# Self-attention's queries and keys as seven half products per two pairs of heads and two batches, with slots in twos

## The chip, the cores and the metric

The kernel runs on one core of one Trainium2 chip. The metric is the device time of one execution in microseconds. The core has five instruction streams: TensorE (PE; its weight loads are listed apart as PEld), VectorE (DVE), ScalarE (ACT), GpSimd (POOL) and SyncE (SP), which issues the DMAs. Each stream runs its instructions in order; an instruction that depends on another engine waits for a semaphore.

## The reference

One decoder block on x of 8 batches, 224 rows, 512 columns, in float32:

1. self-attention: x is RMS-normalised, multiplied by Wq and Wkv (512 to 1024 each for queries, keys and values), split into 16 heads of 64. Queries and keys are divided by their norm over the head's 64 columns and scaled by a gamma. Scores go through tanh(s/50)*50/8 and a softmax over 224 keys, then the weighted values through Wo; x plus the result is layer-normalised.
2. cross-attention to a context of 750 rows, and a layernorm.
3. a gated feed-forward with rounded activations and three-valued weights, and a layernorm.

Only self-attention's queries and keys change here:

```
q = x @ Wq;  k = x @ Wk            # x: normalised, 512 columns; Wq, Wk: 512 x 1024
q = q / max(norm(q), 1e-12) * (gamma_q + 1) * 8   # per head of 64, the same for k
```

## The kernel before, in words

x lives in SBUF as 14 tiles of 128 rows. Self-attention works on groups g of two batches (448 columns of the transposed x, `xnT`; four groups) and on pairs of heads hp (128 columns of Wq or Wk; eight pairs), so on 32 slots m = 8g + hp. All engines but SyncE run in an order that is written out by hand (`manual_schedule`); SyncE's DMAs are placed by the framework where their buffers come free.

One slot m of the loop records, in this order: the weighted values of the slot before (`self_values(m - 1)`: 16 instructions on TensorE, then one multiply on VectorE, L426, into oT); the scores (`self_scores(m)`: 16 on TensorE, then tanh and exp on ScalarE into the two tiles `prs`); `scale_qk(m + 1)` on VectorE (two transposes L313, two multiplies L315); `project_qk(m + 2)` (L263: 32 TensorE instructions of 448 columns, since each float32 matmul stands as two instructions in the trace; ScalarE copies the result and squares it, L287 and L288); `inverse_sums(m)` on VectorE, in two parts (L373 to L404: the softmax's sums and their reciprocals); between its parts `head_norms(m + 2)` (L290: a reduce of the squares L295, four copies L302, two small operations L305 and L306 on VectorE into the tile `nm_q`, then a reciprocal root on GpSimd, L129, into `nm_i`); a value projection (`project_v`, L320) where one is due; a transposition of the normalised x and its copy into xnT (L254, L258) for the next group; an output product through Wo of the group before (`self_output`, L446, and its addition L455 on VectorE); layernorms of what became complete; and the squares, mean squares and scaling of x for the next group.

Buffers that matter: `nm_q` and `nm_o` have one buffer each; `nm_i`, `sq_qk` and other tiles without a number have two; `qk` three. PSUM has three banks under the tag "mm", shared by the projections, the transposed x and the outputs, two double banks for the scores and one bank for the weighted values (`ov_a`). The weights pool has four slots: Wq, Wk, Wv and Wo; at m = 29 the cross-attention's weights are loaded into slots that have come free.

A slot's names in the prediction: Q is `scale_qk`, H is `head_norms`, I is `inverse_sums`, M is the multiply L426. Two slots 2p and 2p + 1 are pair p.

Of the kernel before, what the change touches and what calls it, by code (L numbers as in the profile page):

```python
# [20 lines left out]
F32 = mybir.dt.float32  # L21
BF16 = mybir.dt.bfloat16
AF = mybir.ActivationFunctionType
# [39 lines left out]
def decoder_block(ctx: ExitStack, tc: tile.TileContext, a: dict, out: bass.AP):  # L63
# [47 lines left out]
    wq, wk, wv = ws  # L111
    for i in range(NX // 2, NX):
        load_x(i)
    wo = load_w("attn_Wo", INNER // P, DIM)

    ident = const.tile([P, P], F32, name="ident")
    make_identity(nc, ident)
# [9 lines left out]
    def rsqrt(y, v):  # L127

        nc.gpsimd.tensor_tensor(  # L129
            y, v, mhalf.to_broadcast([P, v.shape[-1]]), ALU.pow  # L130
        )
# [85 lines left out]
    with tc.tile_pool(name="a_sb", bufs=2) as sb, tc.tile_pool(  # L217
# [8 lines left out]
        trs, mms = {}, {}  # L226
# [29 lines left out]
        def copy_xn(i):  # L256
# [3 lines left out]
                ALU.mult,  # L260
            )

        def project_qk(m):  # L263

            for w in range(2):
                block_qk(m, w, (0, G))

        def block_qk(m, w, cols):

            g, hp = divmod(m, NPAIR)  # L270
            c0, c1 = cols
            if (w, c0) == (0, 0):
                qk[m] = sb.tile([P, 2, G], F32, name="qk", bufs=3)
                sq_qk[m] = sb.tile([P, 2, G], F32, name="sq_qk")
            if c0 == 0:
                mms[w] = ps_mm.tile([P, G], F32, tag="mm", name="mm_qk")
            mm = mms[w]
            for k in range(KD):
                nc.tensor.matmul(  # L279
                    mm[:, c0:c1],  # L280
                    lhsT=(wq, wk)[w][:, k, hp * P : (hp + 1) * P],
                    rhs=xnT[:, k, g % 2 * G + c0 : g % 2 * G + c1],
                    start=(k == 0),
                    stop=(k == KD - 1),
                )
            if c1 == G:
                nc.scalar.copy(qk[m][:, w], mm)  # L287
                nc.scalar.activation(sq_qk[m][:, w], qk[m][:, w], AF.Square)  # L288

        def head_norms(m):  # L290

            quarter = sb.tile([P, 4 * NB], F32, name="nm_q", bufs=1)
            nc.vector.tensor_reduce(  # L295
                quarter, sq_qk[m].rearrange("p w (b c) -> p (w b) c", c=Q32), AX.X, ALU.add,
                apply_transpose=True,
            )
# [7 lines left out]
            nc.vector.tensor_scalar(quarter, quarter, 1e-24, None, ALU.max)  # L306
            inv[m] = sb.tile([P, 2, 2 * NB, 1], F32, name="nm_i")
            rsqrt(inv[m].rearrange("p w b o -> p (w b o)"), quarter)

        def scale_qk(m):  # L310
            rb, r = sq_qk.pop(m), inv.pop(m)
            for w in range(2):
                nc.vector.transpose(rb[:, w], r[:, w].to_broadcast([P, 2 * NB, Q32]))  # L313
            for w in range(2):
                nc.vector.scalar_tensor_tensor(  # L315
                    qk[m][:, w], qk[m][:, w], gscale[:, w, m % NPAIR, :], rb[:, w],
                    ALU.mult, ALU.mult,
                )

# [16 lines left out]

        def self_scores(m):

            qT, kT = qk[m][:, 0], qk[m][:, 1]
            scs = []  # L340
            for u in range(2):
                sc = ps_sc.tile([P, 2, 512], F32, name="sc_a")
                sc = sc[:, :, 0 : NT * S].rearrange("p j (t q) -> p j t q", t=NT)
                scs.append(sc)
                for kt, (k0, n) in enumerate(KEYS):
                    for j in range(2):
                        h0, c = j * DH, u * S
                        nc.tensor.matmul(  # L348
                            sc[:n, j, kt, :],
                            lhsT=kT[h0 : h0 + DH, c + k0 : c + k0 + n],  # L350
                            rhs=qT[h0 : h0 + DH, c : c + S],
                            start=True,
                            stop=True,
                        )
# [12 lines left out]

        def inverse_sums(m):


            quarter = sb.tile([P, 2, 2, NB, NT, P // Q32], F32, name="sm_q", bufs=1)
            for u in range(2):
                nc.vector.tensor_reduce(  # L373
                    quarter[:, u, :, :, :, 0].rearrange("p j b t -> p j t b"),
                    prs[u].rearrange("p j t (b c) -> p j t b c", c=Q32),
                    AX.X, ALU.add, apply_transpose=True,
                )


            flat = quarter.rearrange("p u j b t g -> p (u j b t) g")  # L380
            for g in range(1, P // Q32):
                nc.vector.tensor_copy(
                    flat[:Q32, :, g], flat[g * Q32 : (g + 1) * Q32, :, 0]
                )
            yield
            tot = sb.tile([Q32, 2, 2, NB], F32, name="sm_t", bufs=1)
            nc.vector.tensor_reduce(
                tot.rearrange("p u j b -> p (u j b)"),
                quarter[:Q32].rearrange("p u j b t g -> p (u j b) (t g)"), AX.X, ALU.add,
            )  # L390
            isum = sb.tile([P, 2, 2 * NB, 1], F32, name="sm_i", bufs=1)
            for j in range(2):
                nc.vector.reciprocal(
                    isum[:Q32, j, :, 0].rearrange("p (u b) -> p u b", u=2), tot[:, :, j]
                )
            for g in range(1, P // Q32):
                nc.vector.tensor_copy(
                    isum[g * Q32 : (g + 1) * Q32, g // 2, :, 0],
                    isum[:Q32, g // 2, :, 0],
                )  # L400
            rcs[m] = sb.tile([P, 2, S], F32, name="rc_a", bufs=1)
            for j in range(2):
                half = slice(j * DH, (j + 1) * DH)
                nc.vector.transpose(  # L404
                    rcs[m][half].rearrange("p u q -> p (u q)"),
                    isum[half, j].to_broadcast([DH, 2 * NB, Q32]),
                )
            yield

        def self_values(m):  # L410
            g, hp = divmod(m, NPAIR)
# [72 lines left out]
        project_v(0, 0)  # L484
        project_v(1, 0)
        project_qk(1)
        scale_qk(0)
        head_norms(1)
        for i in opened[0][2:]:
            project_v(i, 0)  # L490

        out_at = [(), (0, 2, 4), (0, 2, 4, 6), (4, 5, 6)]
        for m in range(NS):
            g, hp = divmod(m, NPAIR)
            if m > 0:
                self_values(m - 1)
            self_scores(m)
            for i in due:
                scales.append(layernorm([i]))
            due.clear()  # L500
            if m + 1 < NS:
                scale_qk(m + 1)
            if m + 2 < NS:
                project_qk(m + 2)
            sums = inverse_sums(m)
            next(sums)
            if m + 2 < NS:
                head_norms(m + 2)

            c = 1 - hp // 4  # L510
            tiles = opened[g + hp // 4] if g + hp // 4 < NG else ()
            if hp % 4 < len(tiles):
                project_v(tiles[hp % 4], c)
            for _ in sums:
                pass
            for f in scales:
                f()
            scales.clear()
            ahead = opened[g + 1] if g + 1 < NG else ()
# [10 lines left out]
            if 1 <= hp < 1 + len(ahead):  # L530
                scale_x(ahead[hp - 1])
# [22 lines left out]
    dram = ctx.enter_context(tc.tile_pool(name="dram", bufs=1, space=bass.MemoryType.DRAM))  # L554
# [658 lines left out]
```

## Time and profile before

| | before |
|---|---|
| median of 3 runs | 1692.4 us (1692.2 to 1693.05) |
| profiled execution, its own time | 1693.18 us |
| its span, first to last instruction | 1691.4 us |
| granted TensorE clock | 0.999 |
| scores of slot 0 / of slot 31 start | 39.05 / 486.10 us |
| scores to scores, m = 4 to 5, 5 to 6 | 13.47, 13.03 us |
| busy from 38.5 to 143 us: PE, DVE, ACT, POOL | 104.5, 80.1, 65.0, 37.7 of 104.5 us |

A line of the order of time reads: start in us, length, engine, line, operation, output <- input with their shapes, count; in brackets the idle time of the engine just before, and what ended it. Matmuls overlap, so the length of one is not its spacing; the spacing is read from the starts of successive blocks.

### The profile page before, as it was taken

What the parts mean: (1) busy time and instruction counts of PE and PEld (TensorE: products, weight loads), DVE (VectorE), ACT (ScalarE), POOL (GpSimd) and SP (SyncE); (2) the same over time, 40 slices, a digit from 0 to 9 for tenths busy, and PEclk for the clock granted to TensorE, in tenths of its full rate; (3) what the DMA queues carried; (4) which work ended last, traced back from release to release, by engine and by line L of the source; (5) the groups of instructions that cost most, each with busy time, mean ns of one, the idle gap of its engine ahead of it and who ended that gap; (6) DMA issues with size and microseconds to landing.
All of it is one profiled execution on the core that took longest, in us unless ns stands there. A gap on an engine that the chain in (4) does not pass through costs nothing.

```text
span 1691.4 us, 23310 instructions
## 1 busy us (share of the span) xinstructions
PE 1674.4 (99%) x8602; PEld 1076.8 (64%) x8602; DVE 1247.2 (74%) x2776; ACT 879.1 (52%) x1492; POOL 628.9 (37%) x507
## 2 busy tenths in 40 slices
PE   8999999999999999999999999999999999999998
PEld 4555554555546777776776776776776776774443
DVE  3777776767865776776886886897875776886877
ACT  4655544545523664654664664563453544445663
POOL 3333332333411443443443443443443443443244
PEclk9999999999999999999999999999999999999999
DMA  8000000000133222211221121110000000031333
GB/s 286 1 1 1 1 1 1 1 1 1 38 115 109 76 99 75 75 35 38 69 72 38 54 87 38 36 43 7 1 29 3 4 28 1 1 150 30 71 83 105
DMA packets 61956, 80.47 MB, mean 48 GB/s; under 512 B 36753, under 2 KB 38801, under 8 KB 59409
## 3 DMA queue, kind: packets, MB, share of 16 engines
q1 hardware_dynamic: 61840, 78.97, 14.5%
q8 instruction: 68, 1.11, 0.3%
q14 instruction: 48, 0.39, 0.1%
HBM read 60.34 MB, written 9.96 MB: 42 GB/s over the span
## 4 chain that ended last, share of the span: by engine, by line
PE 97%; DVE 1%; DMA 1%; issue 0%; SPq 0%; POOL 0%; POOLq 0%; DVEq 0%
PE mm_k L748 15%; PE mm_v L736 15%; PE mm_qk L279 12%; PE sc_c L785 9%; PE ov_c L879 9%; PE mm_o L446 6%; PE mm_q L761 6%; PE mm_co L194 6%; PE mm_v L325 6%; PE mm_f L1014 5%; PE sc_a L348 3%; PE ov_a L418 3%; PE dn L1102 2%; DMA cT<-ctxT 1%; PE tr_x L254 0%; PE tr_x L719 0%
## 5 line engine op out<-in xcount | busy, mean ns | idle before, releaser
L869 POOL TENSOR_TENSOR csh<-cpT 125x672 f32<-125x672 f32 x128 | 207.4, 1621 | 577.8 <-DVE cpT L859 552.0
L867 ACT ACTIVATE cpT<-cpT 125x1344 f32<-125x1344 f32 x128 | 169.6, 1325 | 228.9 <-DVE cpT L859 220.1
L748 PE MATMUL mm_k<-cT,xattn_Wk 128*128 128x375 f32 x768 | 258.5, 485 | 1.2 <-DMA cT<-ctxT 1.1
L736 PE MATMUL mm_v<-xattn_Wv,cT 128*125 128x256 f32 x1152 | 259.1, 379 | 0.0
L129 POOL TENSOR_TENSOR nm_i<-nm_q,mhalf 128x28 f32<-128x28 f32 x32 | 153.2, 4786 | 271.1 <-DVE nm_q L306 262.5
L736 PEld LDWEIGHTS mm_v<-xattn_Wv,cT 128*125 128x125 f32 x1152 | 216.3, 188 | 28.9
L793 ACT COPY cpT<-sc_c 125x448 f32<-125x448 f32 x384 | 173.7, 561 | 104.2 <-PE sc_c L785 104.1
L748 PEld LDWEIGHTS mm_k<-cT,xattn_Wk 128*128 128x128 f32 x768 | 140.0, 189 | 101.0 <-issue 12.2
L859 DVE TENSOR_TENSOR cpT<-cpT,mx_b 125x1344 f32<-125x1344 f32 x128 | 193.2, 1550 | 2.2
L795 DVE TENSOR_TENSOR cm<-sc_c,cpT 125x448 f32<-125x448 f32 x128 | 73.9, 619 | 146.5 <-ACT cpT L793 146.5
L785 PE MATMUL sc_c<-cqT,ckT 64*125 64x224 f32 x1536 | 163.1, 358 | 0.0
L879 PE MATMUL ov_c<-cpT,cv 125*64 125x224 f32 x1536 | 159.4, 357 | 0.0
L785 PEld LDWEIGHTS sc_c<-cqT,ckT 64*125 64x125 f32 x1536 | 140.3, 184 | 24.7 <-ACT ckT L755 15.0
L879 PEld LDWEIGHTS ov_c<-cpT,cv 125*64 125x64 f32 x1536 | 104.6, 137 | 47.3 <-issue 18.2
L755 ACT COPY ckT<-mm_k 128x375 f32<-128x375 f32 x128 | 59.2, 462 | 126.1 <-PE mm_k L748 126.1
L358 ACT ACTIVATE pr<-sc_a 128x448 f32<-128x448 f32 (+1 forms) x128 | 61.8, 536 | 91.2 <-PE sc_a L348 91.1
L279 PE MATMUL mm_qk<-xnT,wq 128*128 128x448 f32 (+2 forms) x280 | 107.0, 527 | 1.5 <-DVE xnT L258 1.4
L761 PE MATMUL mm_q<-xT,xattn_Wq 128*128 128x224 f32 x512 | 107.1, 352 | 0.0
L761 PEld LDWEIGHTS mm_q<-xT,xattn_Wq 128*128 128x128 f32 x512 | 96.7, 189 | 16.3
L279 PE MATMUL mm_qk<-xnT,wk 128*128 128x448 f32 x256 | 101.5, 539 | 0.0
L325 PE MATMUL mm_v<-wv,xnT 128*128 128x512 f32 x224 | 100.4, 592 | 0.0
L1014 PE MATMUL mm_f<-ternary,xqT 128*128 128x512 bf16 x448 | 98.7, 379 | 0.9 <-DVE x L906 0.9
(131 smaller groups left out, 2530.2 us busy)
## 6 DMA issues: line engine op xcount, KB each, us to landing
cT<-ctxT SPq DMA_DIRECT2D x8, 1125.0 KB, 5.3
w_stage<-w_gateT SPq DMA_DIRECT2D x8, 1024.0 KB, 4.9
w_stage<-w_upT SPq DMA_DIRECT2D x8, 1024.0 KB, 5.1
w_stage<-w_downT SPq DMA_DIRECT2D x8, 1024.0 KB, 5.2
tern<-w_t SPq DMA_DIRECT2D x24, 256.0 KB, 2.0
ternary<-tern SPq DMA_DIRECT2D x3, 2048.0 KB, 12.4
x<-x SPq DMA_DIRECT2D x14, 256.0 KB, 7.4
out<-x SPq DMA_DIRECT2D x14, 256.0 KB, 2.3
```

What stands on the lines that cost most here:

```text
L279: nc.tensor.matmul(mm[:, c0:c1], lhsT=(wq, wk)[w][:, k, hp * P : (hp + 1) * P], rhs=xnT[:, k, g % 2 * G + c0 : g % 2 * G + c1], start=(k = ...
L325: nc.tensor.matmul(mm, lhsT=xnT[:, k, at : at + P], rhs=wv[:, k, c * 512 : (c + 1) * 512], start=(k == 0), stop=(k == KD - 1),)
L736: nc.tensor.matmul(mm[:, i, :], lhsT=cT[:, k, c * CT : (c + 1) * CT], rhs=xwv[:, k, g * VN : (g + 1) * VN], start=(k == 0), stop=(k == KC ...
L748: nc.tensor.matmul(mm, lhsT=xwk[:, k, hp * P : (hp + 1) * P], rhs=cT[:, k, c * HALF : (c + 1) * HALF], start=(k == 0), stop=(k == KC - 1),)
L761: nc.tensor.matmul(mm, lhsT=xwq[:, k, hp * P : (hp + 1) * P], rhs=xT[:, k, :], start=(k == 0), stop=(k == KD - 1),)
L785: nc.tensor.matmul(sc[j][:, i, :], lhsT=kT[h0 : h0 + DH, ct * CT : (ct + 1) * CT], rhs=qT[h0 : h0 + DH, :], start=True, stop=True,)
L793: nc.scalar.copy(pT[:, j, 2 * c2 : 2 * c2 + 2, :], sc[j])
L859: nc.vector.tensor_tensor(pT[:, j], pT[:, j], nm[:CT, j] .rearrange("p (o q) -> p o q", o=1) .to_broadcast([CT, NCT, S]), ALU.add,)
L867: nc.scalar.activation(pT[:, j], pT[:, j], AF.Exp)
L869: nc.gpsimd.tensor_tensor(half, pT[:, j, 0:3], pT[:, j, 3:6], ALU.add)
L879: nc.tensor.matmul(ov[h0 : h0 + DH, :], lhsT=v[:, ct, hq * DH : (hq + 1) * DH], rhs=pT[:, j, ct, :], start=(ct == 0), stop=(ct == NCT - 1),)
L1014: nc.tensor.matmul(mm, lhsT=xqTs[i][:, k, :], rhs=w[:, k, cols], start=(k == 0), stop=(k == KD - 1),)
```

## The change

The products of two pairs of heads (2 x 128 columns of Wq and of Wk) with the two batches of a group are computed as a block product: the contraction of 512 is halved (2 x 256), the weights are halved by the pair of heads, the input by the batch. A 2 x 2 block product by Winograd's form needs seven block products in place of eight, with four sums of weight blocks and four sums of input blocks, and additions of the products. Some of the additions are made in PSUM (a bank `mx` that goes on accumulating after it has been copied out), three on VectorE (`add`, from a second bank `mz`). For each pair j of pairs of heads and group:

- `project_pair(j)` replaces `project_qk(2j)` and `project_qk(2j + 1)`, in five pieces, which the loop puts between the other work of an even slot. The first pair of group 0 is still made as before.
- qk and sq_qk are laid out by batch, then query or key; qk has four buffers.
- `sum_input(g)` makes the four input sums (for group 0 on VectorE, for the others on GpSimd), `sum_weights(jj)` the four weight sums of Wq and of Wk (one set on VectorE, three on GpSimd), and writes them to DRAM.
- In groups 1 to 3 the blocks of a pair are loaded by `load_pair(j)` into one tile, with the sums from DRAM: six DMAs of 128 KB and two of 512 KB each time. Wo is loaded in slot 4 in place of the start.
- Slots go in twos: `scale_qk` runs twice in an even slot, `head_norms` twice in an odd slot, and `inverse_sums` is no longer in parts. In group 1 and 2 the outputs move by a slot, and so do the transpositions.

```diff
-    wo = load_w("attn_Wo", INNER // P, DIM)
+    dram = ctx.enter_context(tc.tile_pool(name="dram", bufs=1, space=bass.MemoryType.DRAM))
...
+        work = wpool.tile([P, 2, 2, 4, KD // 2, P], F32, tag="w", name="w_sums")
+        sums_w = dram.tile([P, NPAIR // 2, 2, 4, KD // 2, P], F32, name="w_sums_all")
+        sums_x = sb.tile([P, 4, KD // 2, S], F32, name="x_sums", bufs=1)
...
+        def sum_weights(jj, eng):
+            for w in range(2):
...
+                eng.tensor_tensor(s1, a21, a22, ALU.add)
+                eng.tensor_tensor(s2, s1, a11, ALU.subtract)
+                eng.tensor_tensor(s3, a11, a21, ALU.subtract)
+                eng.tensor_tensor(s4, a12, s2, ALU.subtract)
+            nc.sync.dma_start(out=sums_w[:, jj], in_=work[:, jj % 2])
...
+        def sum_input(g, eng):
+            b11, b12, b21, b22 = input_blocks(g)
+            t1, t2, t3, t4 = (sums_x[:, i] for i in range(4))
+            eng.tensor_tensor(t1, b12, b11, ALU.subtract)
+            eng.tensor_tensor(t2, b22, t1, ALU.subtract)
+            eng.tensor_tensor(t3, b22, b12, ALU.subtract)
+            eng.tensor_tensor(t4, b21, t2, ALU.subtract)
...
+        def project_pair(j):
+            m = 2 * j
+            open_qk(m)
+            open_qk(m + 1)
+            w = blocks(j)
...
+            yield
+            mx = ps_mm.tile([P, 2, S], F32, tag="mm", name="mm_x")
+            mz = ps_mm.tile([P, 2, S], F32, tag="mm", name="mm_z")
+            def product(mm, first, left, right):
+                for i in range(2):
+                    for k in range(KD // 2):
+                        nc.tensor.matmul(
+                            mm[:, i],
+                            lhsT=w[i][left][:, k],
+                            rhs=right[:, k],
+                            start=first and (i, k) == (0, 0),
+                            stop=(k == KD // 2 - 1),
+                            skip_group_check=True,
+                        )
+            def square_qk(n, u):
+                nc.scalar.activation(sq_qk[n][:, u], qk[n][:, u], AF.Square)
+            def add(n, u):
+                y = qk[n][:, u]
+                nc.vector.tensor_tensor(y, mz, y, ALU.add)
+            product(mx, True, 0, b11)
+            nc.scalar.copy(qk[m][:, 0], mx)
+            product(mz, True, 1, b21)
+            add(m, 0)
+            yield
+            product(mx, False, 4, t2)
+            nc.scalar.copy(qk[m][:, 1], mx)
+            square_qk(m, 0)
+            product(mz, True, 3, t1)
+            product(mx, False, 5, t3)
+            nc.scalar.copy(qk[m + 1][:, 1], mx)
+            yield
+            add(m + 1, 1)
+            yield
+            product(mx, False, 2, t4)
+            nc.scalar.copy(qk[m + 1][:, 0], mx)
+            square_qk(m + 1, 1)
+            square_qk(m + 1, 0)
+            product(mz, False, 6, b22)
+            add(m, 1)
+            square_qk(m, 1)
+            yield
...
         project_qk(1)
+        sum_input(0, nc.vector)
         scale_qk(0)
+        sum_weights(1, nc.vector)
         head_norms(1)
...
-        out_at = [(), (0, 2, 4), (0, 2, 4, 6), (4, 5, 6)]
+        out_at = [(), (1, 3, 5), (1, 3, 5, 6), (4, 5, 6)]
         for m in range(NS):
             g, hp = divmod(m, NPAIR)
+            even = m % 2 == 0
+            pair = project_pair(m // 2 + 1) if even and m + 2 < NS else None
+            step = (lambda: next(pair)) if pair else (lambda: None)
+            step()
+            step()
+            if even and m > 0:
+                scale_qk(m)
             if m > 0:
                 self_values(m - 1)
+            step()
             self_scores(m)
             for i in due:
                 scales.append(layernorm([i]))
             due.clear()
-            if m + 1 < NS:
+            if even:
                 scale_qk(m + 1)
-            if m + 2 < NS:
-                project_qk(m + 2)
-            sums = inverse_sums(m)
-            next(sums)
-            if m + 2 < NS:
+            elif m + 1 < NS:
+                head_norms(m + 1)
                 head_norms(m + 2)
+            step()
+            step()
+            inverse_sums(m)
...
-            for _ in sums:
-                pass
...
-            if 2 <= hp < 2 + len(ahead):
-                transpose_xn(ahead[hp - 2])
-                copy_xn(ahead[hp - 2])
+            if 1 <= hp < 1 + len(ahead):
+                transpose_xn(ahead[hp - 1])
+                copy_xn(ahead[hp - 1])
...
+            if g == 0 and hp in (0, 2, 4):
+                sum_weights((2, 3, 0)[hp // 2], nc.gpsimd)
+            if ahead and hp == 4:
+                sum_input(g + 1, nc.gpsimd)
+            if m >= 4 and even and m + 4 < NS:
+                load_pair(m // 2 + 2)
+            if m == 4:
+                wo = load_w("attn_Wo", INNER // P, DIM)
```

More of the change, by code (lines that the diff above doesn't have):

```diff
@@ L225, in decoder_block @@
         rms_rs = stat.tile([P, NX], F32, name="rms_rs", bufs=1)
-        trs, mms = {}, {}
+        work = wpool.tile([P, 2, 2, 4, KD // 2, P], F32, tag="w", name="w_sums")
+        sums_w = dram.tile([P, NPAIR // 2, 2, 4, KD // 2, P], F32, name="w_sums_all")
+        sums_x = sb.tile([P, 4, KD // 2, S], F32, name="x_sums", bufs=1)
+        trs, mms, loaded = {}, {}, {}
         xn, qk, sq_qk, inv, v, oT, rcs = {}, {}, {}, {}, {}, {}, {}
@@ L261, in copy_xn, with open_qk @@
             )
+        def open_qk(m):
+            qk[m] = sb.tile([P, 2, 2, S], F32, name="qk", bufs=4)
+            sq_qk[m] = sb.tile([P, 2, 2, S], F32, name="sq_qk")
         def project_qk(m):
@@ L268, in block_qk @@
         def block_qk(m, w, cols):
-            g, hp = divmod(m, NPAIR)
             c0, c1 = cols
             if (w, c0) == (0, 0):
-                qk[m] = sb.tile([P, 2, G], F32, name="qk", bufs=3)
-                sq_qk[m] = sb.tile([P, 2, G], F32, name="sq_qk")
+                open_qk(m)
             if c0 == 0:
@@ L280, in block_qk @@
                     mm[:, c0:c1],
-                    lhsT=(wq, wk)[w][:, k, hp * P : (hp + 1) * P],
-                    rhs=xnT[:, k, g % 2 * G + c0 : g % 2 * G + c1],
+                    lhsT=(wq, wk)[w][:, k, m * P : (m + 1) * P],
+                    rhs=xnT[:, k, c0:c1],
                     start=(k == 0),
@@ L286, in block_qk, with blocks @@
             if c1 == G:
-                nc.scalar.copy(qk[m][:, w], mm)
-                nc.scalar.activation(sq_qk[m][:, w], qk[m][:, w], AF.Square)
+                y = qk[m][:, :, w, :]
+                nc.scalar.copy(y, mm.rearrange("p (u q) -> p u q", u=2))
+                nc.scalar.activation(sq_qk[m][:, :, w, :], y, AF.Square)
+        def blocks(j):
+            g, jj = divmod(j, NPAIR // 2)
+            if g:
+                w7 = loaded.pop(j)
+                return [[w7[:, w, i] for i in range(7)] for w in range(2)]
+            return [
+                [
+                    (wq, wk)[w][:, 2 * kh : 2 * kh + 2, (2 * jj + i) * P : (2 * jj + i + 1) * P]
+                    for i, kh in ((0, 0), (0, 1), (1, 1))
+                ]
+                + [work[:, jj % 2, w, i] for i in range(4)]
+                for w in range(2)
+            ]
@@ new lines, in sum_weights @@
+        def sum_weights(jj, eng):
+            for w in range(2):
+                a11, a12, a21, a22 = (
+                    (wq, wk)[w][:, 2 * kh : 2 * kh + 2, (2 * jj + i) * P : (2 * jj + i + 1) * P]
+                    for i in range(2)
+                    for kh in range(2)
+                )
+                s1, s2, s3, s4 = (work[:, jj % 2, w, i] for i in range(4))
+                eng.tensor_tensor(s1, a21, a22, ALU.add)
[3 more added lines that the diff above has]
+            nc.sync.dma_start(out=sums_w[:, jj], in_=work[:, jj % 2])
@@ new lines, in load_pair @@
+        def load_pair(j):
+            jj = j % (NPAIR // 2)
+            if not loaded.get("tile"):
+                loaded["tile"] = [wpool.tile([P, 2, 7, KD // 2, P], F32, tag="w", name="w_pair")]
+            w7 = loaded[j] = loaded["tile"][0]
+            for w, (name, at) in enumerate((("attn_Wq", 0), ("attn_Wkv", 0))):
+                src = a[name].rearrange("(k p) n -> p k n", p=P)
+                for n, (i, kh) in enumerate(((0, 0), (0, 1), (1, 1))):
+                    c = at + (2 * jj + i) * P
+                    nc.sync.dma_start(
+                        out=w7[:, w, n], in_=src[:, 2 * kh : 2 * kh + 2, c : c + P]
+                    )
+                nc.sync.dma_start(out=w7[:, w, 3:], in_=sums_w[:, jj, w])
@@ new lines, in input_blocks @@
+        def input_blocks(g):
+            c = g % 2 * G
+            return [
+                xnT[:, 2 * kh : 2 * kh + 2, c + u * S : c + (u + 1) * S]
+                for kh in range(2)
+                for u in range(2)
+            ]
+        def sum_input(g, eng):
[5 more added lines that the diff above has]
+            eng.tensor_tensor(t4, b21, t2, ALU.subtract)
@@ new lines, in project_pair @@
+        def project_pair(j):
+            m = 2 * j
+            open_qk(m)
+            open_qk(m + 1)
+            w = blocks(j)
+            b11, _, b21, b22 = input_blocks(j // (NPAIR // 2))
+            t1, t2, t3, t4 = (sums_x[:, i] for i in range(4))
+            yield
[11 more added lines that the diff above has]
+                            skip_group_check=True,
+                        )
+            def square_qk(n, u):
[25 more added lines that the diff above has]
+            yield
@@ L295, in head_norms @@
             nc.vector.tensor_reduce(
-                quarter, sq_qk[m].rearrange("p w (b c) -> p (w b) c", c=Q32), AX.X, ALU.add,
-                apply_transpose=True,
+                quarter, sq_qk[m].rearrange("p u w (b c) -> p (u w b) c", c=Q32), AX.X,
+                ALU.add, apply_transpose=True,
             )
@@ L307, in head_norms @@
             inv[m] = sb.tile([P, 2, 2 * NB, 1], F32, name="nm_i")
-            rsqrt(inv[m].rearrange("p w b o -> p (w b o)"), quarter)
+            rsqrt(inv[m].rearrange("p u b o -> p (u b o)"), quarter)
         def scale_qk(m):
             rb, r = sq_qk.pop(m), inv.pop(m)
-            for w in range(2):
-                nc.vector.transpose(rb[:, w], r[:, w].to_broadcast([P, 2 * NB, Q32]))
+            for u in range(2):
+                nc.vector.transpose(
+                    rb[:, u].rearrange("p w q -> p (w q)"),
+                    r[:, u].to_broadcast([P, 2 * NB, Q32]),
+                )
             for w in range(2):
                 nc.vector.scalar_tensor_tensor(
-                    qk[m][:, w], qk[m][:, w], gscale[:, w, m % NPAIR, :], rb[:, w],
+                    qk[m][:, :, w], qk[m][:, :, w], gscale[:, w, m % NPAIR, :], rb[:, :, w],
                     ALU.mult, ALU.mult,
@@ L337, in self_scores @@
         def self_scores(m):
-            qT, kT = qk[m][:, 0], qk[m][:, 1]
             scs = []
@@ L346, in self_scores @@
                     for j in range(2):
-                        h0, c = j * DH, u * S
+                        head = qk[m][j * DH : (j + 1) * DH, u]
                         nc.tensor.matmul(
                             sc[:n, j, kt, :],
-                            lhsT=kT[h0 : h0 + DH, c + k0 : c + k0 + n],
-                            rhs=qT[h0 : h0 + DH, c : c + S],
+                            lhsT=head[:, 1, k0 : k0 + n],
+                            rhs=head[:, 0, :],
                             start=True,
@@ L384, in inverse_sums @@
                 )
-            yield
             tot = sb.tile([Q32, 2, 2, NB], F32, name="sm_t", bufs=1)
@@ L407, in inverse_sums @@
                 )
-            yield
         def self_values(m):
@@ L529, in decoder_block @@
                     rms_norms(ahead[0], ahead[-1] + 1)
-            if 1 <= hp < 1 + len(ahead):
-                scale_x(ahead[hp - 1])
+            if hp < len(ahead):
+                scale_x(ahead[hp])
+            if g == 0 and hp in (0, 2, 4):
[6 more added lines that the diff above has]
+                wo = load_w("attn_Wo", INNER // P, DIM)
             if m == NS - 3:
@@ L553, in decoder_block @@
     parts = const.tile([P, 3, NCHUNK], F32, name="w_parts")
-    dram = ctx.enter_context(tc.tile_pool(name="dram", bufs=1, space=bass.MemoryType.DRAM))
     ternary = [dram.tile([P, NCHUNK, CHUNK], BF16, name=f"tern{i}") for i in range(3)]
```

## The prediction

> **What bounds the kernel now.** I read the busy shares first, then the chain of work that ended last, then TensorE's list of waits up to 530 us, and last the order of time of VectorE and GpSimd in two ordinary slots of self-attention. The page's first part and its chain:
>
> ```profile
> PE 1674.4 (99%) x8602; PEld 1076.8 (64%) x8602; DVE 1247.2 (74%) x2776; ACT 879.1 (52%) x1492; POOL 628.9 (37%) x507
> ...
> PE 97%; DVE 1%; DMA 1%; issue 0%; SPq 0%; POOL 0%; POOLq 0%; DVEq 0%
> ```
>
> TensorE is the end's owner nearly everywhere. Its waits list names 8.5 us over all of self-attention, 7.7 of them before 9 us, so a slot costs what its matmuls cost. VectorE is second, and its stretch of one slot (m=5, start, length, engine, line) shows how little room it has:
>
> ```profile
> 106.74 0.61 DVE L426 TENSOR_TENSOR oT<-ov_a,rc_a 128x448 f32<-128x448 f32 x1
> 108.51 1.17 DVE L313 STREAM_TRANSPOSE sq_qk<-nm_i 128x448 f32<-128x448 f32 x2 [1.16 <-POOL nm_i L129]
> 109.60 1.24 DVE L315 SCALAR_TENSOR_TENSOR qk<-qk,gscale,sq_qk 128x448 f32<-128x448 f32 x2
> 110.76 2.10 DVE L373 TRANSPOSE_TENSOR_REDUCE sm_q<-pr 128x28 f32<-128x896 f32 x2
> 112.89 0.65 DVE L382 COPY sm_q<-sm_q 32x56 f32<-32x56 f32 x3
> 114.70 1.11 DVE L295 TRANSPOSE_TENSOR_REDUCE nm_q<-sq_qk 128x28 f32<-128x896 f32 x1 [1.16 <-ACT sq_qk L288]
> ...
> 116.83 0.18 DVE L306 TENSOR_SCALAR nm_q<-nm_q 128x28 f32<-128x28 f32 x1
> 116.92 0.37 DVE L387 TENSOR_REDUCE sm_t<-sm_q 32x28 f32<-32x224 f32 x1
> ...
> 118.25 1.31 DVE L404 STREAM_TRANSPOSE rc_a<-sm_i 64x448 f32<-64x448 f32 x2
> 119.67 0.62 DVE L426 TENSOR_TENSOR oT<-ov_a,rc_a 128x448 f32<-128x448 f32 x1
> ```
>
> From start to start I take VectorE's pieces: Q (scale_qk) 110.76−108.51 = 2.25; H (head_norms) 116.92−114.70 = 2.2; I (inverse_sums) 2.13+0.66+2.7 = 5.5; M (the multiply of oT) 0.6. That is 10.6 of a 13.0 us slot, and 10.6 of 9.6 us in a slot without project_v, where it falls behind a little and catches up later. GpSimd's order of time gives the length of one reciprocal root (L129) and what follows it:
>
> ```profile
> 117.15 4.78 POOL L129 TENSOR_TENSOR nm_i<-nm_q,mhalf 128x28 f32<-128x28 f32 x1 [8.49 <-DVE nm_q L306]
> 121.89 0.24 POOL L431 COPY oT_tail<-oT 128x64 f32<-128x64 f32 x1
> ```
>
> It starts 0.14 us after H's last instruction ends (117.01), lasts 4.78, and Q starts 0.04 later (121.97): 5.0 us from the end of H to anyone who waits for the root.
>
> [...] Here a 224-column matmul (L761) lasts 352 ns but takes 5.7% of the chain for 512, 188 ns each, the length of its weight load (189); a 448-column one is spaced 375. So halving the columns halves the time, with nothing to spare. [...] L869 (672 elements, 1621 ns) and L870 (224, 667) give 1.14 us for 448 and 0.75 for 256.
>
> **The change, part by part.** *Products.* Two slots' queries and keys were 2 x 32 instructions of 448 columns, 6.12 us a slot (107.21 to 113.33). Now 7 products of 8 instructions of 224 columns: 56 x 188 = 10.53 us. Saved 12.24−10.53 = 1.71 a pair of slots, 25.6 over the 15 pairs changed (pair 0 stays). This alone would give 1667.
>
> *Additions on VectorE.* Three of 128x448 with a PSUM operand, as L426, 0.62 each: 1.9 us a pair. ScalarE keeps four copies and four squares a pair.
>
> *Input and weight sums.* At the start on VectorE, 4 x 0.62 and 8 x about 0.42 (L896, 224 elements, 0.39): they fit into VectorE's 4.9 us of waiting for the root before 27.8 us and 3.3 before 33.5. Uncovered they'd cost 6. On GpSimd three times 8 x 0.75 = 6 us and three times 4 x 1.14 = 4.6; its queue holds H's root behind them. At m=0, 2, 4 and 20 they are done before H ends; at m=12 they wait for the last copy of x and push the root out by 1.8.
>
> *Transfers.* Eight a pair, 1.8 MB; as cT (1125 KB, 5.3 us) some 10 us for the lot. The last two start when the seventh product ends and are wanted about 25 us later. SP's queue holds only the next loads and Wo and xattn_Wk behind them. Nothing, or up to 10 us a pair if late.
>
> *The order.* This decides. In an odd slot head_norms now runs twice in a row. Its tile nm_q has one buffer, and GpSimd's root reads it. So the second H's reduce waits until the first root is done; the built program carries this wait (VectorE's L428 on GpSimd's L129). VectorE stands for 5.0 us, with I(odd), and all after it, behind. Before, Q, I's first half and a whole slot lay between. And TensorE's third product overwrites mm_z, which the first addition A1 must have read: A1 stands behind I(odd).
>
> That closes a ring. From A1's end: 0.1, two products 3.0, scores 1.7, two products 3.0, 0.05 (the last addition needs the seventh product): 7.85. Then on VectorE: addition 0.6, I 5.5, M 0.6, H 2.2, wait 5.0, H 2.2, I 5.5, A1 0.6. Sum 30.05 us a pair. TensorE's own sum with project_v in both slots is 10.53 + scores and values 6.76 + 2 x 3.53 = 24.35, so the ring leads unless an output (6.87) is in the pair.
>
> Added to the ring where they occur: copy of x from the transposition (L258) 0.69, layernorm's scale 0.55, the output's addition 0.69. At m=0, 8, 16 VectorE's mean-square line waits for ScalarE's squares of x, done at 11.4, 12.8 and 11.4 us from the scores' start against 10.9: 0.6, 2.1, 0.6. In slots 9, 11, 17, 19 a transposition and an output follow each other, and with three PSUM buffers the second product gets the one that the transposed x held, so it waits for that copy, which stands after I(odd): then 7.7 us of TensorE (two products' remains, values, three products) come behind it. The layernorm statistics hide in the 2 us before the last addition. In pair 22/23 the output stands in the even slot, and M comes only after it, at 17 us instead of 11; in 28/29 at 13.4.
>
> Scores to scores, pair by pair: 31.4, 31.5, 30.1, 30.1; 37.1, 36.0, 33.7, 30.6; 35.5, 36.0, 31.5, 37.6; 30.1, 30.1, 33.5; the last slot 10.25. Sum 505. The first scores start at 46.6 instead of 39.05 (five products of the first pair now go ahead of them). So the last scores start at 551.6; before at 486.1. What follows is unchanged. +65.5 on the profiled execution (1693.2, span 1691.4): 1758.7; on the median 1692.4: 1757.9. The TensorE gain is inside it: it is swallowed.
>
> **Rivals.** (2) The ring holds but its extras lie in other waits: each pair costs the greater of 30.1 and TensorE's sum (31.8, 31.8, 31.8, 32.2, 31.3 where outputs are). Sum 470, last scores at 517, 1723. For it: I placed each wait by hand. Against: each stands in the in-order queue. (3) VectorE gets slower beside a busier GpSimd, or the weights of a pair come late: some 2 us a pair more, 1775 to 1800. L404 takes 1.31 us both beside a root of GpSimd (118.25) and without one (at 494 us), which speaks against the first. (4) The second H doesn't wait for GpSimd: ring 25.1, and the same list sums to 440.6, last scores at 487.2: 1693.5, no change. (5) The other side: TensorE keeps the lead, 1667. Its one mechanism: the second norm's reduce runs while GpSimd takes the first's root and VectorE's queue drains under TensorE's. It decides once the ring falls below 24.4, 5.7 us shorter, all of the wait and 0.7 more. Nothing in the built order allows it. That the change doesn't do what it says is excluded: the 224-column products are in the built program.
>
> **How the numbers follow.** Chances: walked ring 0.72 (its own range 1744 to 1774, an error of 1 us a pair), (2) 0.11, (3) 0.09, (4) 0.04, (5) 0.04. The range leaves out (4), (5), most of (3) and the lower part of (2): 1730 to 1778. The measurement can tell about 0.2%. Faster: (5) and a quarter of (4), 0.05; same: half of (4), 0.02; slower the rest, 0.93.
>
> **What would show it.** In the profile after: VectorE's reduce of nm_q waits for GpSimd's root, 5.0 us, 15 times; the scores of even slots start 30 us apart at m=4 to 8 (26 before); TensorE is busy for about 25 us less and waits for VectorE's additions and copies of x, some 90 us in all; no transfer in its list of waits above a few us. Wrong if the reduce is seen to start at once, if products are spaced above 188 ns, or if the weights of a pair come after the wait for the additions.

## The result, and the profile after

| | before | after |
|---|---|---|
| median | 1692.3 us | 1805.4 us (1804.2 to 1805.6, 4 runs) |
| ratio | | 1.0666, 95% interval 1.0647 to 1.0684 |
| profiled execution / its span | 1693.2 / 1691.4 us | 1805.4 / 1803.6 us |
| granted TensorE clock | 0.999 | 0.972 |
| scores of slot 0 / of slot 31 start | 39.05 / 486.10 us | 46.01 / 597.99 us |
| between these: all / TensorE busy | 447.0 / 446.9 us | 552.0 / 453.3 us |

The changed kernel is 113 us slower; 65.5 were forecast, and the time lies above the range. The first scores start 7.0 us later than before (7.5 forecast), and the stretch from there to the last scores of self-attention takes 105 us more: 552.0 us where 505 were forecast. From the last scores to the end of the span the two kernels differ by 0.3 us.

The page's first part and the chain that ended last, after:

```profile
PE 1687.3 (94%) x8948; PEld 1163.0 (64%) x8962; DVE 1289.1 (71%) x2833; ACT 872.0 (48%) x1492; POOL 661.7 (37%) x543
...
PE 80%; DVE 12%; POOL 4%; issue 2%; DMA 1%; ACT 0%; SPq 0%; POOLq 0%; DVEq 0%; ACTq 0%
```

TensorE had 97% of the chain and now has 80; VectorE and GpSimd hold 16. TensorE is also busy for 13 us more than before, with half products that should save it 25.6. Both facts matter: the first is the wait that was forecast, the second is what the forecast lacked.

The waits list up to 640 us (engine, its line, whom it waited for; us in all, times, the longest):

```profile
DVE nm_q L428 <- POOL nm_i L129: 85.1, 15, 13.8
PE mm_z L383 <- DVE qk L397: 61.1, 9, 9.4
PE mm_z L383 <- DVE xnT L266: 27.3, 4, 11.8
PE sc_a L483 <- DVE qk L451: 9.8, 1, 9.8
```

The first line is the new wait: fifteen times, one for each odd slot with two norms. The other three are its price on TensorE, 98.2 us. VectorE's order of time in slot 5, which answers to the slot shown of before (start, length, engine, line):

```profile
130.59 1.10 DVE L428 TRANSPOSE_TENSOR_REDUCE nm_q<-sq_qk 128x28 f32<-128x896 f32 x1
...
132.71 0.18 DVE L439 TENSOR_SCALAR nm_q<-nm_q 128x28 f32<-128x28 f32 x1
137.79 1.11 DVE L428 TRANSPOSE_TENSOR_REDUCE nm_q<-sq_qk 128x28 f32<-128x896 f32 x1 [4.91 <-POOL nm_i L129]
...
140.01 2.10 DVE L508 TRANSPOSE_TENSOR_REDUCE sm_q<-pr 128x28 f32<-128x896 f32 x2
...
144.16 1.31 DVE L538 STREAM_TRANSPOSE rc_a<-sm_i 64x448 f32<-64x448 f32 x2
145.50 0.62 DVE L397 TENSOR_TENSOR qk<-mm_z,qk 128x448 f32<-128x448 f32 x1
```

and GpSimd's roots in the same slot:

```profile
132.97 4.79 POOL L129 TENSOR_TENSOR nm_i<-nm_q,mhalf 128x28 f32<-128x28 f32 x1 [2.00 <-DVE nm_q L439]
140.18 4.80 POOL L129 TENSOR_TENSOR nm_i<-nm_q,mhalf 128x28 f32<-128x28 f32 x1 [2.42 <-DVE nm_q L439]
```

The second norm's reduce starts when the first root ends (132.97 + 4.79 = 137.76); the softmax's sums and the first addition (L397, 145.50) are queued behind it, and TensorE stands until the addition is done. What TensorE does then, from its own order of time:

```profile
146.18 3.36 PE L383 MATMUL mm_z<-x_sums,w_pair 128*128 128x224 f32 x8 [5.79 <-DVE qk L397]
149.32 3.13 PE L383 MATMUL mm_x<-x_sums,w_pair 128*128 128x224 f32 x8
152.39 1.78 PE L483 MATMUL sc_a<-qk 64*128 64x224 f32 x16
154.10 1.78 PE L383 MATMUL mm_x<-x_sums,w_pair 128*128 128x224 f32 x8
155.72 1.68 PE L383 MATMUL mm_z<-xnT,w_pair 128*128 128x224 f32 x8
```

Two products of the same eight instructions take 3.14 and 3.07 us from start to start after the wait, and 1.62 and 1.51 from 8 us after its end. TensorE comes out of the wait at half its speed, and the trace's own record of the granted clock says the same. In the table by stretch (length, then busy time and instructions of PE, PEld, DVE, ACT, POOL, then the clock and DMA's share) it stands at 0.50 from 145.44 to 152.26 us, and at 1.00 in the 3.4 us before and after:

```profile
145.44:152.26 6.82, 6.08 (x16) 5.22 (x16) 5.90 (x11) 0.58 (x1) 0.24 (x1) 0.50 0.01 1
```

### The profile page after: what moved, and what is told of

It is laid out like the page before. It is cut to its first block, busy times and chain, and to the rows that moved or that the text cites. A ratio compares the mean times of both kernels' runs of the same rounds, so it can differ in the third digit from the quotient of the medians.

```text
span 1803.6 us, 24283 instructions
## 1 busy us (share of the span) xinstructions
PE 1687.3 (94%) x8948; PEld 1163.0 (64%) x8962; DVE 1289.1 (71%) x2833; ACT 872.0 (48%) x1492; POOL 661.7 (37%) x543
## 4 chain that ended last, share of the span: by engine, by line
PE 80%; DVE 12%; POOL 4%; issue 2%; DMA 1%; ACT 0%; SPq 0%; POOLq 0%; DVEq 0%; ACTq 0%
PE mm_k L897 14%; PE mm_v L885 14%; PE sc_c L934 8%; PE ov_c L1028 8%; PE mm_q L910 5%; PE mm_co L194 5%; PE mm_f L1163 5%; PE mm_z L383 4%; POOL nm_i L129 4%; PE mm_x L383 4%; PE mm_o L579 3%; PE mm_v L461 2%; DVE sm_q L508 2%; PE dn L1251 2%; PE sc_a L483 2%
## 5 line engine op out<-in xcount | busy, mean ns | idle before, releaser
L129 POOL TENSOR_TENSOR nm_i<-nm_q,mhalf 128x28 f32<-128x28 f32 x32 | 153.5, 4798 | 140.2 <-DVE nm_q L439 140.2
L428 DVE TRANSPOSE_TENSOR_REDUCE nm_q<-sq_qk 128x28 f32<-128x896 f32 x32 | 35.4, 1107 | 90.4 <-POOL nm_i L129 85.1
L579 PE MATMUL mm_o<-attn_Wo,oT 128*128 128x512 f32 (+1 forms) x224 | 98.9, 595 | 0.0
L194 PE MATMUL mm_co<-xattn_Wo,coT 128*128 128x512 f32 (+1 forms) x256 | 98.1, 594 | 0.0
```

The source lines that it names most:

```text
L129: nc.gpsimd.tensor_tensor(y, v, mhalf.to_broadcast([P, v.shape[-1]]), ALU.pow)
L194: nc.tensor.matmul(mm[row : row + m, :], lhsT=oT[:, k, at : at + m], rhs=w[:, k, :], start=(k == 0), stop=(k == NPAIR - 1),)
```

## The experiments

The theory after reading the trace, A, is this: nm_q's single buffer makes VectorE wait for GpSimd, TensorE waits for VectorE, and after waits of some length runs at half speed (in this trace after those of 3.69 us and more; after one of 2.22 us the product took the full-speed 1.78 us). Rival B: the new order, or the half products with their sums, cost this by themselves, whatever the buffer.

**e1_nmq2: nm_q in two buffers.**

```diff
-            quarter = sb.tile([P, 4 * NB], F32, name="nm_q", bufs=1)
+            quarter = sb.tile([P, 4 * NB], F32, name="nm_q", bufs=2)
```

> The changed kernel with two buffers for nm_q. Theory A (the second head norm's wait for GpSimd's root is what closes a ring over VectorE, GpSimd and TensorE): VectorE's 85 us of waiting for GpSimd before the reduce of nm_q go to below 5, the ring is 25.1 us a pair, TensorE's waits fall mostly under 3 us and its products come at 188 ns again: 1690 to 1710 us. Theory B (VectorE carries too much work in this order, and another wait takes the place of this one): VectorE's idle time moves to scale_qk or to the additions, 1760 us or more.

Measured: 1716.4 us, ratio 1.0142 (1.0125 to 1.0159). One buffer is 89 of the 113 us; for these the rival falls, and 24 us stay open. No wait of VectorE for nm_q is left. The time is some 6 us above A's range, and 23 above what the prediction gave its rival without the wait. What is left in TensorE's list between 45 and 550 us of e1_nmq2:

```profile
PE mm_z L383 <- DVE qk L397: 19.2, 8, 4.3
PE sc_a L483 <- DVE qk L451: 4.7, 1, 4.7
PE mm_z L383 <- DVE xnT L266: 2.1, 1, 2.1
```

**e2_fill: work for TensorE during the wait.** In eight pairs, 12 or 20 matmuls into a scores bank that nobody reads, put ahead of the product that waits for the first addition.

```diff
             square_qk(m, 0)
+            if j in FILL:      # {2: 20, 3: 12, 4: 12, 5: 20, 9: 12, 13: 20, 14: 12, 15: 20}
+                fill = ps_sc.tile([P, 2, 512], F32, name="sc_a")
+                for n in range(FILL[j]):
+                    nc.tensor.matmul(fill[:, 0, :S], lhsT=w[0][4][:, n % 2],
+                                     rhs=t2[:, n % 2], start=True, stop=True)
             product(mz, True, 3, t1)
```

> The changed kernel with extra matmuls whose result nobody reads, put on TensorE between its second-last finished product and the wait for VectorE's addition, in eight pairs: 12 matmuls (4.5 us) where the wait is 5.5 to 5.9 us, 20 (7.5 us) where it is 8.9 to 9.4. Theory A (TensorE runs at half speed after it has stood idle for some 3 us or more, and that lengthens the ring): in those pairs the two products after the wait take 1.5 us each instead of 3.1, 20 to 25 us less in all, 1780 to 1786 us, with more work. Theory B (those products are slow because of their data, or since VectorE uses the same memory): they stay at 3.1 us, 1805 us or a little more.

Measured: 1794.6 us, ratio 1.0601 (1.058 to 1.0622): 10.8 us faster with more work, about half of what A expected. In seven of the eight filled pairs the products after the wait last 1.78 us and the pair from scores to scores is 1.4 to 3.2 us shorter, 16.7 in all. In the eighth the filling ended 3.16 us too early, and the half speed is back (e2_fill, TensorE's order of time; its lines are numbered one higher here):

```profile
143.76 3.35 PE L384 MATMUL mm_z<-x_sums,w_pair 128*128 128x224 f32 x8 [3.16 <-DVE qk L398]
146.91 3.11 PE L384 MATMUL mm_x<-x_sums,w_pair 128*128 128x224 f32 x8
```

The eighth pair and the unfilled ones lost some 6 us together: in one, a wait that had left the product at full speed in the changed kernel (2.22 us, then 1.78) now gave 3.35 (after 2.23). So the half speed belongs to TensorE's having stood, not to the products; the size expected was too large.

**e3_tail2: oT_tail in two buffers.** In slot 17 GpSimd's copy into oT_tail has to wait for an output product (L579) that still reads the old tail, and the root behind it in the queue, and VectorE behind that. The changed kernel, GpSimd's lines first, then VectorE's:

```profile
352.99 0.24 POOL L564 COPY oT_tail<-oT 128x64 f32<-128x64 f32 x1 [10.64 <-PE mm_o L579]
353.18 4.78 POOL L129 TENSOR_TENSOR nm_i<-nm_q,mhalf 128x28 f32<-128x28 f32 x1
```

```profile
358.00 1.11 DVE L428 TRANSPOSE_TENSOR_REDUCE nm_q<-sq_qk 128x28 f32<-128x896 f32 x1 [13.84 <-POOL nm_i L129]
```

```diff
-                    tails[g] = sb.tile([P, NPAIR, TAIL], F32, name="oT_tail", bufs=1)
+                    tails[g] = sb.tile([P, NPAIR, TAIL], F32, name="oT_tail", bufs=2)
```

> The changed kernel with two buffers for oT_tail. Theory A (in slot 17 GpSimd's copy into oT_tail waits until the output that was moved from slot 16 to 17 has read the old tail, with the root and VectorE's second norm behind it): VectorE's wait there falls from 13.8 to 5.0 us, 1794 to 1798 us. Theory B (the copy of x and TensorE's output set the pace there anyway): below 3 us of gain, 1802 to 1806.

Measured: 1796.0 us, ratio 1.0609 (1.0588 to 1.0631), 9.4 less, as A. The pair of slots 16 and 17 goes from 46.6 to 35.7 us, against 35.5 predicted.

**e4_order8: the order of slots alone.** Everything of the new order stays; the seven half products become four blocks of 448 columns (eight half products' work), with no sums, no additions, and the weights kept on the chip.

```diff
-            product(mx, True, 0, b11)
-            nc.scalar.copy(qk[m][:, 0], mx)
-            product(mz, True, 1, b21)
-            add(m, 0)
+            block(0, 0)          # queries of slot m: eight instructions of 448 columns
             yield
-            product(mx, False, 4, t2)
...
+            block(0, 1)          # its keys
...
+            for w in range(2):   # slot m + 1, after the scores of m
+                block(1, w)
```

> The changed order (slots in twos, two head norms in a row, inverse_sums in one part, outputs and transpositions moved) with the eight products of 448 columns of before, no sums, no additions on VectorE, weights resident, Wo loaded at the start. Theory A (the order with the one-buffer nm_q costs the time): the ring goes from scale_qk over scores, softmax, sums, norm, GpSimd, norm, sums back to scale_qk, about 28 us a pair against 26 for TensorE, 1725 to 1760 us. Theory B (the half products and their additions cost it): 1690 to 1700.

Measured: 1794.8 us, ratio 1.0602 (1.0581 to 1.0623). Both expectations were too low: the order with its one-buffer nm_q costs 102 us with no half product in it. There is no addition to wait for here; TensorE waits for the scaling of the even slot, which stands at the same place behind the second norm (70.6 us in 10 waits in e4_order8), and its scores come out of that at half speed, 3.36 us in place of 1.78.

**e5_nmq2_tail2: both buffers.** The edits of e1_nmq2 and e3_tail2 together.

> Both buffers at once, nm_q and oT_tail with two each; nothing else changed. Theory A (the two waits are separate costs): 1716.4 less the 9.4 us that the tail's second buffer brought by itself, 1705 to 1709. Rival B (GpSimd's root of slot 17 is late in e1_nmq2 too, but VectorE no longer waits for it): 1713 to 1718, no difference from e1_nmq2. In e1_nmq2's list of waits VectorE has no wait for nm_q left, which speaks for B.

Measured: 1713.8 us, ratio 1.0128 (1.011 to 1.0146). B: the tail's buffer is worth nothing measurable once VectorE no longer waits for that root. The costs aren't additive; the late root hurt through nm_q.

**e6_split: both buffers, and the softmax's sums in parts again.** In odd slots the second part of `inverse_sums` runs after the next even slot's `scale_qk`.

```diff
             if even and m > 0:
                 scale_qk(m)
+                next(sums)
...
-            inverse_sums(m)
+            sums = inverse_sums(m)
+            next(sums)
+            if even or m + 1 == NS:
+                next(sums)
```

> As e5_nmq2_tail2, and the sums of the softmax in two parts again, as in the kernel before: in the odd slots the second part, which nothing in TensorE's next products needs, runs after the scaling of the next even slot. Theory A (what is left over the 1692 is the ring of 25.1 us through scaling, scores, additions and norms, against TensorE's 24.35, and the slow products after its waits): the ring loses some 2 to 3 us and TensorE leads, 1670 to 1692, and VectorE's waits for TensorE rise. Rival B (what is left is VectorE beside GpSimd's sums and the output slots): 1703 to 1716, as e5_nmq2_tail2.

Measured: 1713.1 us, ratio 1.0117 (1.0101 to 1.0133): no gain, as B has it, but B's reason is not the one the trace shows. TensorE's waits for an addition are now 16, and 13 of them are for the second one, which had come to stand behind the moved part:

```profile
PE mm_z L383 <- DVE qk L397: 19.8, 16, 3.1
```

**e7_order8_bufs and e8_order8_split: the eight-product order with the same remedies.** e7 is e4_order8 with both buffers, e8 is e7 with the sums in parts.

> e4_order8 (the new order of the slots, but eight products of 448 columns, no sums, no additions, weights kept on the chip) with nm_q and oT_tail in two buffers. Theory A (the order costs only by the wait for nm_q, by what TensorE loses at half speed after it, and by the tail): back to 1692 to 1702. Rival B (putting both slots' work in twos costs by itself, with the wait gone): 1715 to 1760. Against e5_nmq2_tail2 it shows what the seven half products bring or cost in the same order: A expects e5 some 10 us above it, since there the ring has two additions more and GpSimd the sums.

> e7_order8_bufs with the sums of the softmax in two parts as in e6_split: the new order, eight products, no wait for nm_q or for the tail. Theory A: TensorE leads as in the kernel before, 1690 to 1695; e6_split less this one is then what seven half products in place of eight are worth, 0 to 20 us less. Rival B (e6_split gains nothing by its parts either): this one as e7_order8_bufs, and e6_split above it.

Measured: 1720.6 us, ratio 1.0162 (1.0146 to 1.0178), and 1703.3 us, ratio 1.0059 (1.0043 to 1.0075). Neither range of A holds: without the wait the order still costs 28 us, as rival B has it in e7, and 10 with the parts. e7 also lies above e5 and not below it. In e8 TensorE's waits within the stretch are down to 5.6 us, and its clock is 1.00 there, from 45 to 550 us; its first scores start 4.8 us later than before, its last 7.5. What makes up these 10 us is not shown.

**e9_split_add: e6_split with the second addition moved ahead of the odd slot's scaling.**

```diff
             self_scores(m)
+            step()               # add(m + 1, 1)
...
             if even:
                 scale_qk(m + 1)
...
-            step()
             step()
```

> e6_split with one step moved: in even slots the second addition, which the last product waits for, stands ahead of the scaling of the odd slot instead of behind it (2.4 us, 3.4 us beside GpSimd's sums). e6_split had 16 waits of TensorE for an addition, 19.8 us, and 9 us of products slower than 1.7 us a product behind them. Theory A (e6_split gained nothing because its second part of the sums was put ahead of that addition; what keeps the seven products from paying is these waits and what TensorE loses after them): 1683 to 1697, at or below the 1703.3 of the eight products in the same order. Rival B (the waits move to the odd slot's scores, because VectorE is no faster): 1705 to 1715.

Measured: 1688.3 us (1687.2 to 1690.9, 13 runs), ratio 0.9972 (0.9964 to 0.9981), within A's range. It is the only version faster than the kernel before, by 0.28%, and 15.0 us below e8_order8_split, the eight products in this order. Its first part of the page:

```profile
PE 1660.3 (98%) x8948; PEld 1145.4 (68%) x8962; DVE 1288.7 (76%) x2833; ACT 871.9 (52%) x1492; POOL 661.3 (39%) x543
```

VectorE, ScalarE and GpSimd do the work of the changed kernel, to within half a microsecond; only TensorE's busy time differs, by 27.0 us. In the table by stretch, from the first to the last scores, the changed kernel first:

```profile
46.00:598.00 552.00, 453.28 (x2203) 312.48 (x2202) 370.90 (x866) 225.57 (x465) 187.23 (x94) 0.91 0.19 62
```

and e9_split_add:

```profile
46.40:482.50 436.10, 425.90 (x2202) 293.81 (x2200) 371.41 (x869) 225.49 (x465) 186.83 (x94) 0.99 0.24 78
```

The stretches differ by 115.9 us: TensorE stands 98.7 us in one and 10.2 in the other, which makes 88.5, and is busy 27.4 us longer in one with the same instructions. The half products (L383) carry some 26 us of it. The largest part, 9.8 us, lies in those of groups 1 to 3 that wait for the first addition (groups by line, changed kernel, then e9_split_add; busy, mean ns, idle before):

```profile
L383 PE MATMUL mm_z<-x_sums,w_pair 128*128 128x224 f32 x96 | 30.2, 476 | 46.5 <-DVE qk L397 46.5
```

```profile
L383 PE MATMUL mm_z<-x_sums,w_pair 128*128 128x224 f32 x96 | 20.4, 356 | 4.0 <-DVE qk L397 4.0
```

**e10_no_pool_sums: GpSimd's sums left out.**

```diff
                 s1, s2, s3, s4 = (work[:, jj % 2, w, i] for i in range(4))
+                if eng is nc.gpsimd:
+                    continue
...
+        nc.gpsimd.memset(work[:, 0], 0.0)
...
-            if ahead and hp == 4:
-                sum_input(g + 1, nc.gpsimd)
```

The products then read zeros or old sums in their place.

> The changed kernel with GpSimd's sums of weights and inputs left out (24 additions of weights, 12 of inputs; the stores and loads stay, the products read stale sums, so the output is wrong on this point). It prices what GpSimd's sums cost the changed kernel: its root queued behind them in the first pair, and VectorE's copies and scalings at two to three times their time beside them. Theory A (a small term: 3.7 us of slowed VectorE instructions, some 2 us of a late root, and what TensorE loses after the longer waits): 1794 to 1802 in place of 1805.4. Rival B (the sums are a main cause of the missing 46 us): below 1785.

Measured: 1796.3 us, ratio 1.0613 (1.0596 to 1.0631), 9.1 less, as A. The first pair gives 5.3 of it (38.2 to 32.9 us), the pair of slots 12 and 13 another 2.4.

**e11_add_unsplit: the moved addition without the parts.** e5_nmq2_tail2 with the edit of e9_split_add.

> e5_nmq2_tail2 (two buffers for nm_q and oT_tail, the sums of the softmax undivided) with the second addition moved ahead of the scaling of the odd slot, as in e9_split_add. It asks whether that move alone was enough. Theory A (both are needed: with undivided sums TensorE waits for the first addition, which stands behind the whole of them, ring 25.1 us; the second addition is not what it waits for): 1707 to 1716, as e5_nmq2_tail2. Rival B (the move alone does it): 1685 to 1695, as e9_split_add.

Measured: 1716.8 us, ratio 1.0133 (1.0116 to 1.015): A, 0.8 us above its range. TensorE waits for the first addition as in e5 (8 waits, 19.6 us). Each of the two edits alone changes nothing; together they take 25 us.

## Why the prediction was wrong, by its own steps

The direction, the cause and its place were right. The size was not, and the failing step is the ring's term "two products 3.0": behind a long wait the two take up to 6.2 us. The same half speed behind the other long waits included, this is 27 of the 47 us by which the stretch of the scores was forecast too short.

| step | predicted | measured |
|---|---|---|
| wait of the second norm | 5.0 us, 15 times | 15 times: 4.9 to 5.0 us in thirteen, 6.9 in the first pair, 13.8 in slot 17 |
| TensorE waits for additions and copies of x | some 90 us | 88.4 us, and 9.8 us for the scaling before the last even scores |
| first to last scores | 505 us | 552.0 us |
| even slots apart, m = 2 to 8 | 31.5, 30.1, 30.1 us | 34.3, 33.9, 32.2 us |
| slots 16 and 17 | 35.5 us | 46.6 us |
| first pair | 31.4 us | 38.2 us |
| no transfer in TensorE's waits | none above a few us | none |
| TensorE's busy time | 25 us less | 12.9 us more |
| two buffers for nm_q | 1693.5 us (rival 4) | 1716.4 us |

**The two products.** The prediction took 188 ns for each 224-column instruction, and said that spacing above this would show it wrong. After a long wait they are spaced at twice that: 3.14 us for eight. The two that follow the first addition are on the ring, so a pair whose wait is long is up to 3.1 us longer (6.21 in place of 3.13), and the same happens to products that wait for a copy of x and to the last even slot's scores. There are thirteen such waits in the changed kernel, of 3.7 to 11.8 us, and 27.4 us of extra busy time, 2.1 for each; the clock is at half for 99.0 us in all, the later part of the waits included (6.8 us in e9_split_add). The prediction took its 188 ns from a kernel whose granted clock was 0.999, forecast 90 us of waits one after the other, and let the products behind them keep that spacing: an estimate of its author's, which the trace of before did not show. Over the runs, waits of up to 1.79 us were followed by products or scores at full speed (1.78 us after 1.79 in e2_fill), those of 4.31 us or more by ones that were slower, at least in part (2.73 us after 4.31 in e1_nmq2), and between 1.87 and 3.87 us both occurred; the last section has more. e2_fill shows that it is the standing that matters, and e9_split_add that the same instructions take 27 us less without it.

**Full-speed products are also a little longer than 188 ns each.** In an undisturbed pair of e9_split_add the seven products start 1.62, 1.52, 1.60, 1.61, 1.52, 1.51 and 1.61 us before what follows them, 10.99 us in all against 10.53 predicted: 1.6 and not 1.5 where other work comes next or precedes. Over 15 pairs that is 7 us of the 505. The gain of the products in a pair is 1.25 us and not 1.71, so some 19 us in all; against eight products in the same order (e8_order8_split) 15.0 came out.

**Slot 17.** The list of extras put no wait of GpSimd on an output. Moving the output from slot 16 to slot 17 left the old tail in use while GpSimd wanted its only buffer: 9.4 us (e3_tail2).

**"At m=0, 2, 4 and 20 they are done before H ends."** At m=0 GpSimd's sums are not. They start after H has begun, at 58.30, because a root of x's mean squares (`rms_rs`, L129, 57.49) stands ahead of them; H itself takes 4.3 us beside them in place of 2.2, and its root starts at 64.25, 2.1 us after H's end. The changed kernel, VectorE:

```profile
59.00 2.25 DVE L435 COPY nm_o<-nm_q 32x28 f32<-32x28 f32 x4
61.28 0.66 DVE L438 TENSOR_TENSOR nm_q<-nm_q,nm_o 128x28 f32<-128x28 f32 x1
```

In slot 5 these take 0.72 and 0.19 (at 138.94 us). With GpSimd's sums left out (e10_no_pool_sums) the root had nothing ahead of it, stood 1.77 us for H and started at 60.19; here H ends at 62.16. What makes VectorE slower beside the sums was not shown. The prediction had looked at one transposition (L404), saw no difference, and dropped the point. All of GpSimd's sums together are 9.1 us (e10_no_pool_sums), 0.6 a pair: what rival (3) named exists, but at under a third of its 2 us a pair.

The sum of the miss, 47 us: TensorE's standing 98.7 in place of 90, which makes 9, with slot 17 and the first pair in it; its half speed 27; products at full speed 7; some 4 not placed. That is bookkeeping on one trace: the removals above overlap and don't add, as e5 showed for the tail.

**The rivals.** (2) would have had no pair above 32.2 us from even scores to even scores; twelve of the fifteen took more, up to 46.6. (3) has its slower VectorE, at the size just given, and no late weights. (4) came nearest to a test: with the wait gone the ring still leads in pairs without outputs, and TensorE's 8 waits of up to 4.3 us bring back part of the half speed (23.9 us at half clock in e1_nmq2), 1716 in place of 1693.5. (5) said that the ring must lose 5.7 us, the wait and 0.7 more. e9_split_add does that: the second buffer takes the wait, and the parts and the moved addition shorten what TensorE waits for. It ends at 1688 and not at 1667: its undisturbed pairs take 24.8 us from scores to scores (24.35 predicted), some pairs with outputs up to 32.6, and the longest waits left are 3.8 us for a copy of x and 2.0 before the last even scores.

## What to carry to other kernels

Before two uses of a tile are put next to each other, look at how many buffers it has and who reads it last: one buffer of 128x28 cost this kernel 89 us. Price a wait of TensorE by its length: those of 3.69 us or more cost their time here and on the mean 2.1 us of half speed behind each (27.4 us over thirteen), up to 3.1, so many waits on a ring cost more than the ring's sum. In the profile, read the granted clock of a stretch right behind a wait, not only its mean over the span. When a reordering has to pay by a few per cent of TensorE's work, follow each engine's queue for a whole period, since here two edits that did nothing alone took 25 us together.

## What the runs showed of the hardware that was not expected

- Half speed after waits: eight 224-column float32 instructions in 3.1 us in place of 1.5, sixteen instructions of scores 3.36 in place of 1.78. At 1.87 to 3.87 us of waiting it isn't decided by the length alone: 3.85 us left the product at full speed in e11_add_unsplit, 2.23 gave half speed in e2_fill.
- In the changed kernel's trace the granted clock is full or half, never between, and up to 620 us each stretch at half clock lasts 3.41, 6.83, 10.24 or 13.65 us: one, two, three or four times 3.41. Cut the time from 42 to 620 us into pieces of 3.41 us that start where these stretches do, and take the 140 pieces at full clock by how long TensorE stood within them: the 127 with at most 1.93 us were followed by full clock, the 13 with 2.42 us or more by half. Of the 29 pieces at half clock, the 13 with at most 0.44 us were followed by full clock, the 16 with 0.74 us or more by another at half. The two waits of 2.2 us show the same (tables by stretch: two such pieces of the changed kernel, then two of e2_fill). The first wait is split over two pieces, with 1.83 us of it in one and the clock at 1.00 in the next; the second, 2.23 us, lies in one, and the clock in the next is 0.50:

```profile
288.80:292.21 3.41, 1.58 (x8) 1.23 (x7) 3.21 (x10) 0.53 (x1) 1.98 (x1) 1.00 0.02 3
292.21:295.62 3.41, 3.02 (x16) 2.95 (x16) 3.37 (x7) 0.58 (x1) 0.00 (x0) 1.00 0.00 0
```

```profile
286.35:289.76 3.41, 1.18 (x8) 0.83 (x6) 3.24 (x10) 0.53 (x1) 1.59 (x1) 1.00 0.00 0
289.76:293.17 3.41, 3.41 (x9) 3.12 (x10) 3.37 (x6) 0.58 (x1) 0.00 (x0) 0.50 0.00 0
```

- VectorE's operations beside GpSimd's additions, in the changed kernel: four copies of 32x28 took 2.25 us (at 59.00) in place of 0.72, two scalings of 128x448 took 2.22 (at 82.04) in place of 1.28 (at 113.65). GpSimd's own addition of 128x256 went from 0.73 (at 81.17) to 1.10 us (at 83.74) beside such a scaling.
